# First-block loads and VectorE order, block 1's value weights, and the output's operand loads in an attention and expert-bottleneck kernel

## The chip, the cores and the metric

The kernel runs on one core of a Trainium2 chip. The metric is the device time of one execution in microseconds, taken as the median of several runs. The engines are TensorE (PE, its weight loads PEld), VectorE (DVE), ScalarE (ACT), GpSimd (POOL) and SyncE (SP), which here issues most DMAs; ScalarE issues the others on a queue of its own.

## The reference, cut to what matters

```python
x  = L0_attn_x                                # (2, 2048, 2048) float32, 4096 tokens
xn = (x - mean(x)) / sqrt(var(x) + 1e-5)
qkv = xn @ Wqkv + bqkv                        # Wqkv: 2048 x 1536; q, k, v of 512 each
out = softmax(q @ k.T / sqrt(512)) @ v        # for each of the 2 batches
attn = out @ Wo + bo                          # Wo: 512 x 2048
scores = (xn @ Wq_w.T) @ keys.T               # 16 router dimensions, 64 experts
gate = softmax over the 16 highest scores, zero elsewhere
z = (xn @ A_w.T) * gate                       # 64 experts x rank 8 = 512
result = x + attn + (z @ B_w.T) * 2.0
```

## The kernel before

All large products are float32 products made of three fp32r matmuls: each operand is split into a high part, which ScalarE casts (`split_hi`, L123), and a low part, the difference, which VectorE (or GpSimd, if told so) subtracts (`split_lo`, L126). `product` (L131) adds low x high, high x low and high x high into one PSUM bank. There are seven banks `acc` and one `misc`.

The 4096 tokens are eight blocks of 512, each of four row tiles of 128. Blocks 0 and 1 are computed directly; blocks 2 to 7 in three pairs (`phase`, seven products for eight); then come the scores and the weighted sums of attention, and last the output product in the same seven-product form, in 16 rounds q of seven steps (P1, P2, P6, P5, P3, P7, P4). Rounds 0 to 7 make the first 1024 output columns (p = 0), rounds 8 to 15 the other 1024 (p = 1).

**Block 0** (`first_block`, L321). TensorE is warmed with bf16 matmuls on a zero tile. For each row tile t: `load` brings 128 rows of x; `normal` takes statistics on VectorE (four `bn_stats`, L196, and one aggregate), then -mean (`nm`) and variance plus eps (`ve`), and GpSimd the reciprocal root (`rs`, L190); `scale` normalizes three quarters of the rows on VectorE (L351) and the fourth on ScalarE (L355, L356); `turn` transposes 16 squares of 128 on TensorE (L365) and splits them into `xh`. Value and router weights come as eight pieces (c2) of 256 rows for each half h of 264 columns (`wv_piece`, `weights`: load into `ws`, of which there are four buffers, high part, low part into `wh`, of which there are eight). `mul` (L378) is six matmuls 128x264 for one row tile and one piece. In the kernel before, the first half's pieces have their low parts on GpSimd; the first four are loaded by ScalarE's queue, the x rows by SP.

`values_out` (L274) empties a value bank: ScalarE copies the router's 16 columns (L282) and casts the high part (L286), VectorE subtracts (L287), and a store to DRAM is put down for later (`store`); `flush` issues what was put down. The buffers `vs` come from the ring `r_ev` of three.

**Block 1's values** (`values`, L299) run over the halves h, in each over the eight pieces, the two 128-row chunks of a piece and the four row tiles, one bank for each row tile. In the half h = 1 a step of block 2's statistics goes with each piece (`steps`: ScalarE's queue loads 1024 columns of x into one of three buffers `xs`, VectorE takes statistics).

**The feature tiles** of blocks 0 and 1 (L851 on) are 12 products of 48 matmuls each (`ftile`). At given tiles (`todo`, L862) they carry steps for later blocks, among them four loads of block 2's part of xT (`x_steps`, L628, 512 KB each).

**The output.** `moving(p, step, kk)` (L1064) returns a pair: `load`, which brings a step's weights into `r_wo` (two buffers) or, for the small steps of p = 1, `r_wo1` (four), and `split`, which makes high and low parts (`wb`) in the four slots of that step. Those slots are in use by the same step of the round before. `ahead` (L1209) prepares the other operand `s` three products ahead, `stationary` (L1112) with VectorE's sums and differences of `xz` (L1119 to L1124). `combine` (L1177): P1's bank is copied to `u` by ScalarE (L1182) and then P2 accumulates on the same bank.

What sets the order: each engine runs its instructions in the order in which the program was built, and a scheduler of the tile layer chose that order by estimated readiness when the kernel was built. `behind(key)` (L113) ties what is traced inside it behind a remembered instruction (`last[key]`) on that instruction's engine; instructions on other engines aren't tied. A DMA takes one of eight completion lanes in turn, and an issue waits for the DMA before it on its lane.

The lines that the change touches, beside those printed below:

```python
862            with behind("sp", "pe"):
863                for st in todo.get(k, []):
864                    st()
...
927    nc.vector.memset(mr32, 0.0)
930    nc.vector.memset(raw(mhl), 0.0)
932    nc.vector.tensor_tensor(pick, ...)
...
1300            m = n + 7 * q - 7 * (NG - 1)
1301            if 0 <= m < 7:
1302                more[m] = [moving(1, STEPS[m], kk) for kk in range(0, ND, 2)]
1303                for load, _ in more[m]:
1304                    load()
1305            if 1 <= m <= 7:
1306                with behind("act"):
1307                    for _, split in more[m - 1]:
1308                        split()
```

Of the kernel before, what the change touches and what calls it, by code (L numbers as in the profile page):

```python
# [34 lines left out]
def raw(ap):  # L35
    return ap.bitcast(F32)
# [27 lines left out]
def attn_ffn_kernel(ctx: ExitStack, tc, x, xT, wq, wv, wob, bqk, bv, bo, keysT, out):  # L64
# [57 lines left out]
    def split_hi(hi, src):  # L122
        return nc.scalar.copy(hi, src)  # L123
# [150 lines left out]
    def values_out(i, t, h, r, qr, ps, u=None):  # L274

        n0 = RD if h == 0 else 0
        at = 0 if h == 0 else VH - RD
        vs = r([P, 2, VH], FR, "vs")
        if u is None:
            v = ps  # L280
            if h == 0:
                nc.scalar.copy(qr[:, t, :RD], ps[:, :RD])  # L282
        else:
            v = raw(vs[:, 1, :])
            nc.vector.tensor_tensor(v[:, n0:], ps[:, n0:VH], u[:, n0:], ALU.add)
        split_hi(vs[:, 0, n0:], v[:, n0:VH])  # L286
        split_lo(vs[:, 1, n0:], v[:, n0:VH], vs[:, 0, n0:])  # L287
        store(v_d[i][t][:, :, at : at + VH - n0], raw(vs[:, :, n0:]))

    def wv_piece(h, c2, eng=None, queue=None):  # L290
        ch, cc = divmod(2 * c2, HC)
        return weights(wv[h, ch, :, cc : cc + 2, :], [2, VH], eng, queue)
# [6 lines left out]
    def values(i, xn, steps):  # L299
        qr = router_in()  # L300
        for h in range(2):
            ps = [acc() for t in range(NT)]
            for c2 in range(NCH // 2):
                wh = wv_piece(h, c2)
                for cc in range(2):
                    c = 2 * c2 + cc
                    for t in range(NT):
                        sl = slice(t * P, (t + 1) * P)
                        product(
                            ps[t][:, :VH], lambda a: xn[c][:, a, sl], lambda b: wh[:, b, cc, :],  # L310
                            c == 0, c == NCH - 1,
                        )
                if h == 1:
                    with behind("sp", "pe", "dve"):
                        steps[c2]()
            flush()
            for t in range(NT):
                values_out(i, t, h, r_ev, qr, ps[t])
        return qr

    def first_block():  # L321
# [8 lines left out]
        def load(t, cols):  # L330
            rows[t] = [xs0[2 * t + c]([P, 1024], F32, "xs") for c in range(2)]
            for c in range(2):
                for h in range(1024 // cols):
                    a = h * cols
                    nc.sync.dma_start(
                        rows[t][c][:, a : a + cols],
                        x[t * P : (t + 1) * P, c * 1024 + a : c * 1024 + a + cols],
                    )

        def normal(t):  # L340
            st = const.tile([P, 4, 6], F32, name="st6", bufs=2)
            row_stats(mv[:, t, :], rows[t], 0, st)
            nc.vector.tensor_scalar(nm[:, t : t + 1], mv[:, t, 0:1], -1.0, None, ALU.mult)
            rstd(rs[:, t : t + 1], mv[:, t, 1:2], 1)

        def scale(t):
            for n in range(4):
                c, h = divmod(n, 2)
                v = rows[t][c][:, h * 512 : (h + 1) * 512]
                if n < 3:  # L350
                    nc.vector.tensor_scalar(  # L351
                        v, v, mv[:, t, 0:1], rs[:, t : t + 1], ALU.subtract, ALU.mult
                    )
                else:
                    nc.scalar.activation(v, v, AF.Identity, bias=nm[:, t : t + 1])  # L355
                    nc.scalar.mul(v, v, rs[:, t : t + 1])  # L356

        def turn(t, g0=0, g1=NCH // 4):
            sl = slice(t * P, (t + 1) * P)
            for g in range(g0, g1):  # L360
                pt = acc()
                for j in range(4):
                    c = 4 * g + j
                    k = (c % 8) * P
                    nc.tensor.transpose(pt[:, j * P : (j + 1) * P], rows[t][c // 8][:, k : k + P], ident)  # L365
                for part in range(2):
                    for j in range(4):
                        hi, lo = (xn[4 * g + j][:, a, sl] for a in range(2))
                        pj = pt[:, j * P : (j + 1) * P]
                        if part == 0:  # L370
                            split_hi(hi, pj)
                        else:
                            split_lo(lo, pj, hi)

        def piece(c2, h, eng=None, queue=None):
            return wv_piece(h, c2, eng, queue)
# [11 lines left out]
        warm = half(0)([P, T], mybir.dt.bfloat16, "warm")  # L388
        nc.vector.memset(warm, 0.0)
        pw = misc()  # L390
        for j in range(20):
            nc.tensor.matmul(pw, warm[:, :P], warm, start=True, stop=True)
        load(0, 512)
        wh = [piece(c2, 0, nc.gpsimd, nc.scalar) for c2 in range(2)]
        normal(0)
        scale(0)
        load(1, 1024)
        turn(0, 0, 2)
        normal(1)
        turn(0, 2, 4)  # L400
        ps = [acc() for t in range(NT)]
        mul(ps[0], wh[0], 0, 0)
        mul(ps[0], wh[1], 0, 1)
        wh.append(piece(2, 0, nc.gpsimd, nc.scalar))
        mul(ps[0], wh[2], 0, 2)
        scale(1)
        wh.append(piece(3, 0, nc.gpsimd, nc.scalar))
        load(2, 1024)
        turn(1)
        for c2 in range(3):  # L410
            mul(ps[1], wh[c2], 1, c2)
        wh += [piece(c2, 0, nc.gpsimd) for c2 in range(4, N2)]
        load(3, 1024)
        constants()
        for c2 in range(3, N2):
            mul(ps[0], wh[c2], 0, c2)
            mul(ps[1], wh[c2], 1, c2)
            if c2 == 4:
                normal(2)
                scale(2)  # L420
                turn(2)
                normal(3)
        qr = router_in()
        for t in range(2):
            values_out(0, t, 0, r_ev, qr, ps[t])
# [405 lines left out]
    for i in range(2):  # L831
# [19 lines left out]
        for k, (fp, fh, summed) in enumerate(order):  # L851
# [43 lines left out]
    for j in PAIRS:  # L895
# [34 lines left out]
    nc.vector.memset(raw(mhl), 0.0)  # L930
    pick = const.tile([32 + NQ, NQ], F32, name="pick")
    nc.vector.tensor_tensor(
        pick, ident[: 32 + NQ, :NQ], ident[: 32 + NQ, 32 : 32 + NQ], ALU.add
    )

    def score(s):
        blk, k = divmod(s, NK)
# [338 lines left out]
    for q in range(2 * NG):  # L1276
# [4 lines left out]
        for n, step in enumerate(STEPS):  # L1281
# [69 lines left out]
```

## Time and profile before

| what | us |
|---|---|
| runs shown: lowest, median, highest of 3 | 2654.17, 2660.54, 2663.89 |
| the profiled execution's own time | 2656.96 |
| its span, first to last instruction | 2655.2 |
| VectorE busy in the span | 1807.5 |
| ScalarE busy in the span | 863.1 |
| GpSimd busy in the span | 569.6 |
| mean granted TensorE clock | 0.997 |

How to read it: a row of the timeline has the start, the duration, the engine, the line, the operation, what it writes and reads, how many instructions are merged, and in brackets how long the engine stood idle before it and what ended that. A row of the windows has a stretch, its length, the busy time (and number of instructions) of PE, PEld, VectorE, ScalarE and GpSimd, the granted clock of TensorE as a share of full speed, the mean busy share of the 16 DMA engines, and GB/s. Times are counted from the span's start. Beside the profile, the order in which the built programs hold each engine's instructions was read for both kernels; it has no times.

### The profile page before, as it was taken

The numbers are of one execution on the slowest core, as the hardware profiler recorded it, in microseconds if no ns is written. First come the engines' busy times: TensorE is split into PE (matmuls) and PEld (weight loads), VectorE is DVE, ScalarE is ACT, GpSimd is POOL, SyncE is SP. The second block draws the span as 40 slices with busy tenths as digits, with TensorE's granted clock in tenths as the row PEclk, the third lists the DMA queues.
The fourth block names the chain that finished last, engine by engine and source line by source line (L and its number), as shares of the span: only waits on it lengthen the run. The fifth ranks groups of instructions, "written<-read, shape, count | busy, mean of one in ns | idle before, by whom it ended". The sixth has DMA issues, their size and how long they took to land.

```text
span 2655.2 us, 33831 instructions
## 1 busy us (share of the span) xinstructions
PE 2628.8 (99%) x12875; PEld 2224.7 (84%) x12875; DVE 1807.5 (68%) x2487; ACT 863.1 (33%) x1285; POOL 569.6 (21%) x355
## 2 busy tenths in 40 slices
PE   8998999999999999999999999999999999999999
PEld 7888888888888888888888888888888888878887
DVE  6667738867878687756545675466568776797675
ACT  4232323333332333323233342334344222332221
POOL 2311420000000000000100101000002656556654
PEclk9999999999999999999999999999999999999999
DMA  6777775668546784536735476534368545565543
GB/s 232 252 259 264 269 264 201 212 211 298 194 143 220 233 299 137 175 115 213 289 116 178 155 254 237 206 119 143 125 202 270 172 161 165 181 212 174 178 158 105
DMA packets 243395, 530.42 MB, mean 200 GB/s; under 512 B 21608, under 2 KB 87200, under 8 KB 243232
## 3 DMA queue, kind: packets, MB, share of 16 engines
q1 hardware_dynamic: 229984, 497.81, 55.6%
q10 hardware_dynamic: 13248, 30.45, 3.3%
q8 instruction: 101, 1.65, 0.3%
q14 instruction: 62, 0.51, 0.1%
HBM read 393.80 MB, written 134.38 MB: 199 GB/s over the span
## 4 chain that ended last, share of the span: by engine, by line
PE 92%; DVE 4%; DMA 3%; issue 1%; ACT 0%; POOL 0%; SPq 0%; DVEq 0%; ACTq 0%; POOLq 0%
PE acc L131 69%; PE acc L1170 22%; DMA xs<-in_x 2%; DVE st L196 1%; DMA ws<-in_wv 1%; DMA xc<-in_xT 1%; DVE pw L126 1%; DVE xc L256 1%; DVE xq L655 1%; DVE wh L126 0%; DVE xc L257 0%; DVE t L126 0%; DVE wb L126 0%; DVE xs L351 0%; DVE s L126 0%
## 5 line engine op out<-in xcount | busy, mean ns | idle before, releaser
L131 PE MATMUL acc<-t,pw 128*128 128x512 f32 x3024 | 694.3, 390 | 1.1 <-DVE t L126 0.9
L131 PEld LDWEIGHTS acc<-t,pw 128*128 128x128 f32 x3024 | 565.3, 188 | 119.6 <-DVE t L126 1.8
L1170 PE MATMUL acc<-wb,s 128*128 128x512 f32 x2688 | 609.7, 389 | 2.6 <-ACT u L1182 2.6
L1170 PEld LDWEIGHTS acc<-wb,s 128*128 128x128 f32 x2688 | 504.6, 188 | 107.5 <-ACT u L1182 3.0
L131 PE MATMUL acc<-ph,vt 128*128 128x512 f32 x1536 | 367.5, 390 | 0.0
L131 PE MATMUL acc<-qt,kt 128*128 128x512 f32 x1536 | 366.0, 389 | 0.0
L131 PEld LDWEIGHTS acc<-ph,vt 128*128 128x128 f32 x1536 | 287.5, 188 | 62.1 <-DVE ot L1033 1.2
L131 PEld LDWEIGHTS acc<-qt,kt 128*128 128x128 f32 x1536 | 288.2, 188 | 60.2 <-issue 0.2
L1154 POOL TENSOR_TENSOR xo<-xo,bo_bc 128x512 f32<-128x512 f32 x128 | 212.6, 1667 | 560.4 <-DMA xo<-in_x 305.1
L123 ACT CAST pw<-pw 128x1024 fp32r<-128x1024 f32 (+1 forms) x168 | 177.6, 1058 | 378.9 <-PE acc L131 219.9
L131 PE MATMUL acc<-xh,wh 128*128 128x512 f32 x1152 | 263.6, 390 | 0.0
L126 DVE TENSOR_TENSOR pw<-pw 128x1024 fp32r<-128x1024 f32 (+1 forms) x168 | 217.2, 1293 | 67.5 <-ACT pw L123 67.1
L131 PEld LDWEIGHTS acc<-xh,wh 128*128 128x128 f32 x1152 | 215.6, 188 | 44.9
L131 PEld LDWEIGHTS acc<-pw,t 128*128 128x128 f32 x2016 | 245.8, 188 | 1.3
L131 PE MATMUL acc<-pw,t 128*128 128x264 f32 x2016 | 246.4, 283 | 0.0
L123 ACT CAST s<-xz 128x1024 fp32r<-128x1024 f32 x112 | 118.0, 1054 | 381.8 <-PE acc L1170 305.0
L126 DVE TENSOR_TENSOR s<-xz,s 128x1024 fp32r<-128x1024 f32 x112 | 168.0, 1500 | 43.9 <-ACT s L123 43.8
L126 DVE TENSOR_TENSOR ph<-sp,ph 128x512 fp32r<-128x512 f32 x128 | 94.2, 738 | 120.4 <-ACT ph L123 119.6
L957 DVE TENSOR_TENSOR M<-M,sp 128x512 f32<-128x512 f32 x112 | 79.3, 708 | 124.1 <-ACT sp L951 123.6
L525 POOL TENSOR_TENSOR zt<-zt,g 128x512 f32<-128x512 f32 x24 | 34.3, 1441 | 494.6 <-DMA g<-gd 203.8
L951 ACT COPY sp<-acc 128x512 f32<-128x512 f32 x128 | 74.8, 585 | 183.2 <-PE acc L131 183.1
L126 DVE TENSOR_TENSOR wh<-wu,wh 128x512 fp32r<-128x512 f32 x96 | 85.4, 906 | 70.5 <-ACT wh L123 70.5
(150 smaller groups left out, 2383.7 us busy)
## 6 DMA issues: line engine op xcount, KB each, us to landing
vt<-v_d SPq DMA_DIRECT2D x128, 512.0 KB, 3.5
pw<-sq_d SPq DMA_DIRECT2D x72, 512.0 KB, 3.7
xz<-oz_d SPq DMA_DIRECT2D x64, 512.0 KB, 4.9
xo<-in_x SPq DMA_DIRECT2D x128, 256.0 KB, 3.5
out_y<-xo SPq DMA_DIRECT2D x128, 256.0 KB, 2.3
pw<-in_wq SPq DMA_DIRECT2D x54, 512.0 KB, 3.7
wu<-in_wq SPq DMA_DIRECT2D x48, 512.0 KB, 7.0
xq<-in_xT SPq DMA_DIRECT2D x48, 512.0 KB, 5.7
```

Of the source, the lines that this page charges most:

```text
L123: return nc.scalar.copy(hi, src)
L126: return (eng or nc.vector).tensor_tensor(lo, src, raw(hi), ALU.subtract)
L131: last["pe"] = nc.tensor.matmul(ps, st(a_), mv(b_), start=first and n == 0, stop=end and n == 2)
L196: nc.vector.bn_stats(st[:, parts, :], xt[:, h * 512 : (h + 1) * 512])
L256: nc.vector.tensor_tensor(xc, xc, mb[:, 0, :], ALU.subtract)
L525: nc.gpsimd.tensor_tensor(zt, zt, gx[n], ALU.mult)
L655: eng.tensor_tensor(xg[(j, *to, cp)], xg[(j, *x0, cp)], xg[(j, *x1, cp)], op)
L951: nc.scalar.copy(st, ps)
L957: nc.vector.tensor_tensor(M[blk], M[blk], st, ALU.max)
L1154: nc.gpsimd.tensor_tensor(xs, xs, bo_bc[q // (NB // 2 * NH), c], ALU.add)
L1170: nc.tensor.matmul(ps, st[a_][:, kk, sl], mv[b_], start=not more and kk == 0 and n == 0, stop=kk == ND - 1 and n == 2, skip_group_check=more,)
```

## The change

In block 0 the second half of the first row tile's columns is loaded by ScalarE's queue, 26 warm-up matmuls take the place of 20, the low parts of pieces 0 to 5 are subtracted by VectorE (6 and 7 still by GpSimd), and the order on VectorE is written out with `behind`. In block 1 the pieces of the second half, but for the first, are tied behind the last eviction of the first half. The steps of `todo` are also tied behind the last issued store. Three small VectorE operations for attention are tied behind the last weight subtraction. In the output, the weights of the second column half are loaded two products before they are split.

```diff
@@ values_out
-        split_hi(vs[:, 0, n0:], v[:, n0:VH])
+        last["ev"] = split_hi(vs[:, 0, n0:], v[:, n0:VH])
@@ values
-                wh = wv_piece(h, c2)
+                with behind(*(["ev"] if h == 1 and c2 else [])):
+                    wh = wv_piece(h, c2)
@@ first_block: load, normal, scale, turn
-                    nc.sync.dma_start(
+                    (nc.scalar if t == 0 and c else nc.sync).dma_start(
...
-            nc.vector.tensor_scalar(nm[:, t : t + 1], mv[:, t, 0:1], -1.0, None, ALU.mult)
+            last["nm"] = nc.vector.tensor_scalar(nm[:, t : t + 1], mv[:, t, 0:1], -1.0, None, ALU.mult)
...
-                    nc.vector.tensor_scalar(
+                    last["row"] = nc.vector.tensor_scalar(
...
-                            split_lo(lo, pj, hi)
+                            last["row"] = split_lo(lo, pj, hi)
@@ first_block
-        for j in range(20):
+        for j in range(26):
             nc.tensor.matmul(pw, warm[:, :P], warm, start=True, stop=True)
         load(0, 512)
-        wh = [piece(c2, 0, nc.gpsimd, nc.scalar) for c2 in range(2)]
+        wh = [piece(0, 0, None, nc.scalar)]
         normal(0)
+        with behind("nm"):
+            wh.append(piece(1, 0, None, nc.scalar))
         scale(0)
         load(1, 1024)
         turn(0, 0, 2)
-        normal(1)
+        for c2 in range(2, 4):
+            with behind("row"):
+                wh.append(piece(c2, 0, None, nc.scalar))
         turn(0, 2, 4)
         ps = [acc() for t in range(NT)]
-        mul(ps[0], wh[0], 0, 0)
-        mul(ps[0], wh[1], 0, 1)
-        wh.append(piece(2, 0, nc.gpsimd, nc.scalar))
-        mul(ps[0], wh[2], 0, 2)
+        for c2 in range(3):
+            mul(ps[0], wh[c2], 0, c2)
+        with behind("row"):
+            normal(1)
+        with behind("nm"):
+            wh += [piece(c2, 0) for c2 in range(4, 6)]
         scale(1)
-        wh.append(piece(3, 0, nc.gpsimd, nc.scalar))
         load(2, 1024)
+        for c2 in range(3, 6):
+            mul(ps[0], wh[c2], 0, c2)
         turn(1)
-        for c2 in range(3):
+        for c2 in range(6):
             mul(ps[1], wh[c2], 1, c2)
-        wh += [piece(c2, 0, nc.gpsimd) for c2 in range(4, N2)]
+        with behind("row"):
+            wh += [piece(c2, 0, nc.gpsimd) for c2 in range(6, N2)]
         load(3, 1024)
         constants()
-        for c2 in range(3, N2):
+        for c2 in range(6, N2):
             mul(ps[0], wh[c2], 0, c2)
             mul(ps[1], wh[c2], 1, c2)
-            if c2 == 4:
-                normal(2)
+            if c2 == 6:
+                with behind("row"):
+                    normal(2)
                 scale(2)
                 turn(2)
-                normal(3)
+                with behind("row"):
+                    normal(3)
@@ feature tiles
-            with behind("sp", "pe"):
+            with behind("sp", "pe", "store"):
@@ before attention
-    nc.vector.memset(mr32, 0.0)
+    with behind("dve"):
+        nc.vector.memset(mr32, 0.0)
...
@@ output
             if 0 <= m < 7:
-                more[m] = [moving(1, STEPS[m], kk) for kk in range(0, ND, 2)]
-                for load, _ in more[m]:
+                with behind("act"):
+                    for _, split in more.pop(m):
+                        split()
+            if -2 <= m < 5:
+                more[m + 2] = [moving(1, STEPS[m + 2], kk) for kk in range(0, ND, 2)]
+                for load, _ in more[m + 2]:
                     load()
-            if 1 <= m <= 7:
-                with behind("act"):
-                    for _, split in more[m - 1]:
-                        split()
```

The memset of `mhl` and the operation `pick` (L930, L932) are tied in the same way as `mr32`.

More of the change, by code (lines that the diff above doesn't have):

```diff
@@ L926, in attn_ffn_kernel @@
     mr32 = const.tile([P, 32], F32, name="mr32")
-    nc.vector.memset(mr32, 0.0)
+    with behind("dve"):
+        nc.vector.memset(mr32, 0.0)
     mrT = const.tile([P, 32], F32, name="mrT")
     mhl = const.tile([32 + NQ, 32], FR, name="mhl")
-    nc.vector.memset(raw(mhl), 0.0)
+    with behind("dve"):
+        nc.vector.memset(raw(mhl), 0.0)
     pick = const.tile([32 + NQ, NQ], F32, name="pick")
-    nc.vector.tensor_tensor(
-        pick, ident[: 32 + NQ, :NQ], ident[: 32 + NQ, 32 : 32 + NQ], ALU.add
-    )
+    with behind("dve"):
+        nc.vector.tensor_tensor(
+            pick, ident[: 32 + NQ, :NQ], ident[: 32 + NQ, 32 : 32 + NQ], ALU.add
+        )
     def score(s):
```

## The prediction

> **What bounds it now.** I read the page's first part, then what TensorE waited for, then windows and timeline around those waits.
>
> ```profile
> PE 2628.8 (99%) x12875; PEld 2224.7 (84%) x12875; DVE 1807.5 (68%) x2487; ACT 863.1 (33%) x1285; POOL 569.6 (21%) x355
> ```
>
> TensorE is busy 99% of the span, so a change that removes no matmul can win only TensorE's idle time and its slow clock. The list of what PE waited for (total us, times, longest) gives the places:
>
> ```profile
> PE acc L131 <- DVE vs L126: 9.4, 1, 9.4
> PE acc L365 <- DVE xs L351: 7.6, 3, 6.3
> PE acc L1170 <- ACT u L1182: 2.6, 1, 2.6
> ```
>
> They are block 1's second value half (at 229 us), the first row tile, and the output's second product of q = 8 (at 2349 us). The change touches all three. The windows (PE busy, PEld, DVE, ACT, POOL, granted clock, DMA share, GB/s) show that a long wait also costs clock:
>
> ```profile
> 6.00:8.00 2.00, 1.86 (x9) 0.66 (x7) 1.38 (x2) 0.74 (x2) 2.00 (x2) 1.00 1.09 402
> ...
> 12.00:14.00 2.00, 0.00 (x0) 0.00 (x0) 2.00 (x4) 0.00 (x0) 1.22 (x2) 0.62 1.01 411
> ```
> ```profile
> 233.00:236.00 3.00, 0.00 (x0) 0.00 (x0) 2.81 (x5) 1.67 (x6) 0.00 (x0) 0.72 0.95 338
> 236.00:239.00 3.00, 0.22 (x1) 0.22 (x2) 2.97 (x8) 1.22 (x6) 0.00 (x0) 0.50 0.89 307
> 239.00:242.00 3.00, 3.00 (x14) 3.00 (x15) 2.93 (x8) 0.37 (x1) 0.00 (x0) 0.50 0.88 296
> 242.00:245.00 3.00, 3.00 (x17) 3.00 (x16) 0.91 (x3) 0.62 (x1) 1.81 (x2) 0.57 0.67 207
> ```
>
> A mean of 0.72 over 3 us is 1.7 us at half clock, 0.57 is 2.6: the clock was half from 234.3 to 244.6, having fallen 5.0 us after TensorE stopped at 229.3. Likewise it fell 4.6 us after the warm-up matmuls end (7.87), at 12.5, and came back at 19.3.
>
> **Part 1, block 1 (values_out, values).** The timeline:
>
> ```profile
> 235.56 0.37 ACT L123 CAST vs<-acc 128x248 fp32r<-128x248 f32 x1
> ...
> 238.78 6.39 PE L131 MATMUL acc<-wh,xh 128*128 128x264 f32 x29 [9.44 <-DVE vs L126]
> ...
> 241.32 0.37 ACT L123 CAST vs<-acc 128x248 fp32r<-128x248 f32 x1 [4.10 <-DMA v_d<-vs]
> ```
>
> The second half's first nine matmuls use three spare banks; the fourth must be evicted. In the built order ScalarE has six weight casts of the second half ahead of the evictions, each waiting for its load, so the eviction starts at 235.5. In the changed order the four evictions come directly behind the first cast. Bank 0 is complete 9 matmuls (1.1 us) before the first half's end; copy, cast and VectorE's subtraction take 0.9 us (50.17 to 51.07 for the same operations in block 0). The bank is then free when it is needed. Removed: 9.44 us idle, and of the 5.8 us from 238.78 to 244.6 at half clock half, 2.9 us: 12.3.
>
> What is late next is the second piece. Its cast now stands behind the fourth eviction, whose buffer is the first's (three slots) and waits for the first's store: issue to cast took 238.75 to 241.32, 2.57 us. Counted from the first half's end: store issued at 0, fourth cast 2.6 to 3.0, weight cast 0.63 to 3.6, subtraction 0.70 to 4.3. TensorE wants it after 24 matmuls of 0.1216 (201 took 24.44), 2.9. New wait 1.4 us, too short for the clock. Later pieces cost VectorE 0.70 + two statistics 1.28 + 0.13 = 2.1 us against TensorE's 2.9. The four 512 KB loads of xT that lay among these weights (209 to 219 us) go behind a store, two feature tiles later; four tiles of 10.9 us lie before their use, so they cost nothing; without that room, one landing (5.7 us on the page). **Gain 12.3 - 1.4 = 10.9**; ends 7 (store landing in 5 us) and 12.3.
>
> **Part 2, the first row tile.**
>
> ```profile
> 13.63 1.43 DVE L351 TENSOR_SCALAR xs<-xs,mv,rs 128x512 f32<-128x512 f32 x3
> 14.20 3.27 PEld L365 LDWEIGHTS acc<-ident,xs 128*128 128x128 f32 x16 [6.84 <-DVE xs L351]
> 14.21 3.67 PE L365 MATMUL acc<-ident,xs 128*128 128x128 f32 x16 [6.34 <-DVE xs L351]
> ...
> 15.36 3.34 ACT L123 CAST xh<-acc 128x128 fp32r<-128x128 f32 x16 [3.68 <-PE acc L365]
> ```
>
> Before, the four quarters landed at 4.8, 6.0, 7.3, 8.6, each beside a weight piece; 0.53 MB per 1.3 us is what the DMA gives. Now quarters share that rate with quarters: all in by 6.0, statistics end at 7.8 instead of 9.8, and the statistics of tile 1 no longer stand before the scaling. But two weight subtractions, new on VectorE, do. Their pieces come behind the quarters, beside 512 KB rows on the other queue. Their queue's share is not shown there; where such pairs run together (231 to 233 us) I read some 0.4. Pieces land at 7.8, 9.8, 11.7, 13.3 (with half: the last at 12.0; with a third: 14.6). Second piece 9.8 + cast 0.63 + subtraction 0.70 = 11.1, scaling 0.57: first transpose 11.7 instead of 14.2. The warm-up, six more at 0.21, ends at 9.15: 2.5 us idle, clock kept.
>
> Then it is given back. ScalarE's fourth weight cast stands before the sixteen xh casts: 13.3 + 0.63 = 13.9 (15.36 before). VectorE starts 0.8 later, 16 x 0.20 + two weight pieces 1.3: 19.2, where before it ended at 19.7. Only now come tile 1's statistics (four 2.46, then 0.5), two more pieces 1.3, scaling 0.6: tile 1's transposes run from 24.1 to 26.0; before, they ended at 26.8. Gain so far 0.8 (2.1 with half, -0.6 with a third). POOL's rs(1) stands behind pieces 6 and 7 there, whose loads are last in the queue; done near 22.9, covered by the 23.5; if they land 2 us later, tile 1 slips by 1.4.
>
> Next, tile 3. VectorE's new order puts the eviction of ps[2] before tile 3's nm and ve. All of ps[2] must therefore finish first, and TensorE has nothing else queued before tile 3's transposes. From the end of ps[2]: 0.15 + eviction 0.9 + nm, ve 0.2 + POOL 0.65 + scaling 0.6 = 2.5 us idle, where before matmuls of ps[2] covered the same chain. Against some 0.3 us of small waits saved there: -2.2. **Part 2: 0.8 - 2.2 = -1.4**; ends -5 (third share, and half clock, below) and +5 (transposes 2.5 earlier plus half of 14.2 to 19.3, nothing given back).
>
> One new gap may cost clock. Tile 0's matmuls with pieces 4 and 5 wait for VectorE from about 18.3 (pieces 2 and 3 done at 17.6, six matmuls each) to 22.9: 4.6 us, and the clock fell 4.6 and 5.0 us after work stopped. I count it as not falling; if it falls, it stayed half for 5.1 and 5.8 us after work resumed, 2.9 at most, some 2 beside the other waits. [...]
>
> On the two queues the rows show both busy from the start (share 1.09, 402 GB/s); only who goes first changes. [...]
>
> **Part 3, output.**
>
> ```profile
> 2348.29 1.72 DVE L1122 TENSOR_TENSOR xz<-xz 128x1024 f32<-128x1024 f32 x1
> ...
> 2350.11 1.04 ACT L123 CAST s<-xz 128x1024 fp32r<-128x1024 f32 x1 [9.72 <-DVE xz L1122]
> 2351.07 1.07 ACT L1182 COPY u<-acc 128x512 f32<-128x512 f32 x2
> ...
> 2351.70 4.61 PE L1170 MATMUL acc<-wb,s 128*128 128x512 f32 x19 [2.56 <-ACT u L1182]
> ```
>
> The bound is VectorE's backlog (3.00 of 3.00 in every window from 2329), not loads: from 2285 on VectorE waited 0.2 us for a weight cast and for no load. The built order moves the first u copy ahead of the s cast, so P2's first tile starts on time; the second stays behind it. VectorE's L1122 moves behind four halves of P7's weights, one of P4's and a finish. Net from the end of P3's weights (2342.7, less 2.4 for three operations that moved behind it): 11.2 us of listed work, L1122 from 2351.5 to 2352.8, cast 1.05, copy 0.6: P2's second tile near 2354.7 instead of 2351.9. Tile 2 would before have started at 2351.7 + 2.73 = 2354.4. **About -0.7** with some POOL overlap (ops of 1.2 stretch to 2.2 here); ends +2.6 (wait gone) and -4: on SP the loads of a step now wait for the split two products back, before the xo loads and the stores of out, and VectorE, which waited 1.8 us for xo here, would wait for those.
>
> The three memsets and pick go from the first 13 us to before attention: 1.1 us on an engine at 68%, nothing; at worst 1.1.
>
> **Sum.** 10.9 - 1.4 - 0.7 = 8.8 us. The profiled execution took 2656.96 (span 2655.2 and 1.8 around it): 2648.2. It lies 3.6 under the median of the runs shown, 2660.54; the forecast is for that median: **2651.7**.
>
> **Rivals.** (a) The start does pay: pieces land at equal share, little is given back, +4, and the output breaks even: gain 15, 2645.5. For: everything on VectorE is ordered for tile 0. Against: the tile-3 wait above. (b) More is given back: the 4.6 us gap halves the clock (-2) and the store lands late in block 1 (-3.5): gain 3.3, 2657.2. (c) Slower: block 1's pieces become a serial loop. Each x load now stands between two weight casts on ScalarE and waits for statistics of a load three back; before, casts came at 222.5, 226.0, 229.2, 3.3 us apart, with DMA at 1.05. If a loop takes 5 us against TensorE's 2.9, seven pieces lose 14.7, and net with parts 2 and 3 it is 12.3 - 14.7 - 2.1 = -4.5: 2665.0. It decides from 4.4 us a piece on. Against: the xT loads are gone from there, so 0.79 MB a piece needs 2 us. (d) That the order is not what the diff says: excluded by the built order.
>
> **Chances.** Forecast 0.53 (2648 to 2656), (a) 0.25, (b) 0.15, (c) 0.06, rest 0.01. For 8 in 10: 2643 to 2658. Half a per cent, 13.3 us, is about what a measurement of this kernel can tell from no change: faster 0.24 (most of (a)), same 0.72, slower 0.04 (the far end of (c)).
>
> **What would show it.** No PE wait on vs L126 at 229 and no half clock there; one of 1 to 2 us soon after. First transpose near 11.7, tile 1's ending near 26, a PE wait of 2 to 3 us on tile 3's scaling; P2's second output tile waiting on u. Wrong if pieces land much earlier than 13, if tile 3 does not wait, or if any new wait passes 4.6 us.

## The result, and the profile after

The changed kernel took 2662.2 us (median of 22 runs, 2657.3 to 2667.45); the kernel before took 2656.84 in as many (2653.66 to 2663.89). The ratio is 1.0017, with a 95% interval of 1.001 to 1.0024: some 3 to 6 us slower, where 8.8 us less had been forecast, and 4 us above the range. The forecast stood on the median of the three runs known then, 2660.54; on the median of all 22 it would have been 2648.0. Measured against the 0.5% bound the result is no change; against its own interval it is a small loss.

The profiled execution has a span of 2661.1 us (2655.2 before). The engines' line of its page, and then the list of what TensorE waited for (total us, times, longest):

```profile
PE 2632.8 (99%) x12881; PEld 2227.1 (84%) x12881; DVE 1818.6 (68%) x2493; ACT 863.4 (32%) x1285; POOL 569.7 (21%) x349
```
```profile
PE acc L1184 <- ACT u L1196: 7.7, 1, 7.7
PE acc L366 <- DVE xs L352: 5.1, 1, 5.1
PE acc L131 <- DVE wh L126: 4.6, 1, 4.6
PE acc L366 <- issue: 2.4, 1, 2.4
PE acc L131 <- ACT t L123: 1.8, 1, 1.8
```

The wait of 9.4 us in block 1 is gone. In its place the output's wait has grown from 2.6 to 7.7, the first row tile has a second wait of 4.6, and two smaller ones are new. TensorE is also "busy" 4.0 us more. The 26 warm-up matmuls took 7.24 us, the 20 before 6.68: 0.6 of that. A matmul at half clock counts as busy for nearly twice as long (before, 26 of 128x264 took 5.50 us from 239.0 on at half clock, 85 took 10.00 from 206 on at full: 0.21 and 0.12 each); TensorE worked 18.0 us at half clock, against 10.9 before, and half of the difference, 3.5, is about the rest.

Both traces hold every matmul, so the start of the n-th one behind the warm-up can be compared between them. This splits the 5.9 us between the two executions by place:

| from, to | difference at the end of the stretch | in the stretch | forecast |
|---|---|---|---|
| start to tile 3's transposes (42.31 us before, 49.00 after) | +6.7 | +6.7 | +1.4 |
| to block 1 at full clock (244.63, 240.22) | -4.4 | -11.1 | -10.9 |
| to pair 1's second product at full clock (537.7, 536.6) | -1.1 | +3.3 | 0 |
| to the output's q = 8, ahead of its wait (2345.1, 2343.8) | -1.4 | -0.3 | 0 |
| to the end | +5.9 | +7.3 | +0.7 |

Block 1, in the timeline (start, duration, engine, line, operation, and in brackets the idle time ahead and what ended it):

```profile
237.57 0.37 ACT L123 CAST vs<-acc 128x248 fp32r<-128x248 f32 x1 [2.26 <-DMA v_d<-vs]
...
238.52 11.66 PE L131 MATMUL acc<-wh,xh 128*128 128x264 f32 x92 [0.53 <-ACT wh L123]
```

The fourth eviction waits for the first's store, as forecast, and the weight cast behind it makes TensorE wait; but for 0.53 us, not 1.4.

The first row tile, in the same view:

```profile
9.72 0.63 ACT L123 CAST wh<-ws 128x528 fp32r<-128x528 f32 x1 [2.84 <-DMA ws<-in_wv]
...
13.55 3.67 PE L366 MATMUL acc<-ident,xs 128*128 128x128 f32 x16 [5.13 <-DVE xs L352]
...
21.30 2.46 DVE L196 BATCH_NORM_STATS2 st<-xs 128x6 f32<-128x512 f32 x4
...
24.23 2.01 DVE L126 TENSOR_TENSOR wh<-ws,wh 128x528 fp32r<-128x528 f32 x2
...
25.67 2.79 PE L131 MATMUL acc<-wh,xh 128*128 128x264 f32 x11 [4.64 <-DVE wh L126]
...
28.26 3.48 PE L366 MATMUL acc<-ident,xs 128*128 128x128 f32 x16
```

The first weight piece is cast at 9.7 instead of the forecast 7.8, and the transposes come at 13.55 instead of 11.7. Pieces 4 and 5, cast by 19.9, are subtracted from 24.2 on, behind tile 1's statistics, and the first of the two takes 1.39 us, where the two at 18.48 took 0.70 each, while GpSimd's subtraction for piece 7 runs until 25.06 beside it; TensorE stands for 4.64 us until then. Sixteen transposes take 3.5 us at 28.26 where 1.9 is usual: the clock is half. The windows (PE busy, PEld, DVE, ACT, POOL, granted clock, DMA share, GB/s) show it there and in the output:

```profile
21.00:25.60 4.60, 0.03 (x1) 0.00 (x0) 4.53 (x11) 1.99 (x3) 3.10 (x3) 0.90 0.41 124
25.60:31.50 5.90, 5.83 (x28) 5.83 (x28) 3.35 (x12) 2.71 (x12) 0.44 (x1) 0.50 0.94 308
...
2350.00:2358.00 8.00, 0.51 (x3) 0.08 (x1) 8.00 (x6) 1.34 (x2) 6.57 (x5) 0.66 0.36 131
```

In the first row VectorE is busy 4.53 of 4.60 us and the DMAs are at 0.41: the list, not a load, holds TensorE. The last row says the same of the output, with GpSimd busy beside VectorE. What TensorE waits for there is the forecast chain, the second copy to `u` behind the cast of `s`, and that cast behind VectorE's sum of `xz` (L1136; L1122 in the kernel before):

```profile
2356.66 1.05 ACT L123 CAST s<-xz 128x1024 fp32r<-128x1024 f32 x1 [10.89 <-DVE xz L1136]
2357.61 0.58 ACT L1196 COPY u<-acc 128x512 f32<-128x512 f32 x1
...
2358.24 17.12 PE L1184 MATMUL acc<-wb,s 128*128 128x512 f32 x65 [7.74 <-ACT u L1196]
```

### The profile page after: what moved, and what is told of

It is laid out like the page before. It is cut to its first block, busy times and chain, and to the rows that moved or that the text cites. A ratio compares the mean times of both kernels' runs of the same rounds, so it can differ in the third digit from the quotient of the medians.

```text
span 2661.1 us, 33841 instructions
## 1 busy us (share of the span) xinstructions
PE 2632.8 (99%) x12881; PEld 2227.1 (84%) x12881; DVE 1818.6 (68%) x2493; ACT 863.4 (32%) x1285; POOL 569.7 (21%) x349
## 4 chain that ended last, share of the span: by engine, by line
PE 95%; DVE 2%; DMA 2%; issue 1%; ACT 0%; ACTq 0%; SPq 0%; DVEq 0%
PE acc L131 73%; PE acc L1184 22%; DMA xs<-in_x 1%; DVE wb L126 1%; DMA ws<-in_wv 0%; DVE st L196 0%; DVE pw L126 0%; PE acc L366 0%; DVE xq L666 0%; DMA wo<-tw_d 0%; DVE xo L1173 0%; PE misc L466 0%; PE misc L999 0%; DVE xh L126 0%; DVE wh L126 0%
## 5 line engine op out<-in xcount | busy, mean ns | idle before, releaser
L126 DVE TENSOR_TENSOR wh<-wu,wh 128x512 fp32r<-128x512 f32 x96 | 96.1, 1025 | 64.9 <-ACT wh L123 64.9
```

What stands on the lines that cost most here:

```text
L126: return (eng or nc.vector).tensor_tensor(lo, src, raw(hi), ALU.subtract)
```

## The experiments

The theory after the result: the three parts are independent and add; the start loses by its queue's share, by VectorE's order and by the clock; the output loses because VectorE's list reaches one sum of `xz` later. Times are medians; ratios are against runs of the kernel before on the same chip.

| run | us | ratio, 95% interval |
|---|---|---|
| e1: block 1's part alone | 2646.59 | 0.9959, 0.9947 to 0.9972 |
| e2: first block's part alone | 2668.1 | 1.0042, 1.003 to 1.0055 |
| e3: output's part alone | 2663.24 | 1.0024, 1.0015 to 1.0033 |
| e4: block 1's part and the store tie | 2645.63 | 0.9956, 0.9943 to 0.9968 |
| e5: changed kernel, pieces 4, 5 first | 2659.41 | 1.0004, 0.9996 to 1.0013 |
| e6: changed kernel, pieces on one queue | 2656.41 | 0.9995, 0.9986 to 1.0004 |
| e7: changed kernel, no bias at q = 8 | 2656.82 | 1.0, 0.9992 to 1.0009 |
| e8: e4, longer warm-up, late cast | 2651.2 | 0.9979, 0.997 to 0.9988 |
| e9: changed kernel, splits one product later | 2655.17 | 0.9986, 0.9977 to 0.9995 |
| e10: e4 with a repaired first block | 2646.93 | 0.9958, 0.9946 to 0.9971 |
| e11: e10 with four low parts on GpSimd | 2641.13 | 0.9941, 0.9929 to 0.9954 |
| e12: the changed kernel once more | 2661.55 | 1.0014, 1.0005 to 1.0024 |

### The parts, each alone (e1 to e4)

e1 is the kernel before with this alone:

```diff
-        split_hi(vs[:, 0, n0:], v[:, n0:VH])
+        last["ev"] = split_hi(vs[:, 0, n0:], v[:, n0:VH])
...
-                wh = wv_piece(h, c2)
+                with behind(*(["ev"] if h == 1 and c2 else [])):
+                    wh = wv_piece(h, c2)
```

> Block 1's part alone: the weight pieces of its second half stand behind the last eviction, nothing else of the change. In the two profiles the changed kernel won 11.1 us between matmul 1250 and matmul 1277 (block 1) and lost 3.4 again at about 531 us, where pair 1's second product starts (1.8 + 0.9 us of waits and a stretch of 3.41 us at half clock). Theory: the win is block 1's alone, and the loss at 531 us is what VectorE and the loads take back from any kernel that arrives early there: no wait over 1.5 us at 229 us, a wait of 1 to 3 us near 530 us, and 7 to 9 us less than before (ratio 0.997). Rival A: the loss at 531 us comes from the moved xT loads, which this kernel doesn't have: 10 to 12 us less (0.9958). Rival B: without the room in the queue that the moved xT loads made, a weight piece comes late and block 1 itself waits some 5.7 us again: 2 to 6 us less.

Measured 2646.59, ratio 0.9959: Rival A's number. Between the same two matmuls in block 1 its profile gains 11.1 us, the wait there is 0.60 us, and nothing is lost near 530 us. So the loss of 3.3 at that place is not what any kernel that arrives early gives back, as the theory had it, and rival B falls too: the xT loads may stay where they were.

e2 is the kernel before with all that the change's diff has under `first_block`, and nothing else:

```diff
+                    (nc.scalar if t == 0 and c else nc.sync).dma_start(
...
+        for j in range(26):
...
+        wh = [piece(0, 0, None, nc.scalar)]
...
+        with behind("row"):
+            normal(1)
+        with behind("nm"):
+            wh += [piece(c2, 0) for c2 in range(4, 6)]
```

> The first block's part alone (row quarters on two queues, 26 warm-up matmuls, VectorE's subtractions and order). In the two profiles it lost 6.7 us by the end of tile 3's wait: first transpose only 0.7 earlier, then 4.6 us without matmuls and half clock from 24.6 to 31.5 us, then 2.1 us before tile 3. Theory: the loss is its own: 5 to 7 us more than before (ratio 1.002 to 1.0026), less up to 1.4 of it if the small waits at 534 us vanish. Rival: most of it was where the clock's windows happened to fall in that one execution: 1 to 3 us more (1.0008), with no half clock after 24 us in this profile.

Measured 2668.1, ratio 1.0042: more than the theory's 5 to 7. The start lost 6.4 us by tile 3's transposes, as in the changed kernel, with half clock again (from 23.8 to 30.6 us). The rest comes later: 1.1 in block 1, whose wait became 10.3, 1.5 at pair 1's second product (a wait of 1.6 us on `t`), and 1.6 from half clock behind the output's old wait.

e3 is the kernel before with the output's hunk of the diff alone:

```diff
             if 0 <= m < 7:
-                more[m] = [moving(1, STEPS[m], kk) for kk in range(0, ND, 2)]
...
+                with behind("act"):
+                    for _, split in more.pop(m):
+                        split()
+            if -2 <= m < 5:
+                more[m + 2] = [moving(1, STEPS[m + 2], kk) for kk in range(0, ND, 2)]
```

> The output's part alone (weights of the second column half loaded two products ahead). In the two profiles it lost 7.0 us: TensorE waits 7.74 us for the first product's copy of q = 8 (2.56 before) and runs at half clock for some 4.5 us behind that. Theory: VectorE's sums of xz come later because their order now has six halves of weights ahead of them and GpSimd's bias adds run beside these, so the loss is the edit's own: 5 to 9 us more than before (ratio 1.002 to 1.003). Rival: the loss came from the 3 to 4 us that the changed kernel is ahead there, with the loads where they were: 0 to 2 us more.

Measured 2663.24, ratio 1.0024, and a wait of 7.9 us for u: the theory. The kernel is not ahead there (2.6 us behind in this profile), so the loss doesn't come from being early.

e4 is e1 with one more line:

```diff
-            with behind("sp", "pe"):
+            with behind("sp", "pe", "store"):
```

> Block 1's part and the tie of the steps behind the last store (which moves four 512 KB loads of xT from among block 1's weights to the feature tiles). Theory: the tie is worth nothing either way: within 1.5 us of the kernel with block 1's part alone, and the same wait near 530 us. Rival A: the tie is what loses at 531 us: 3 to 4 us slower than block 1's part alone. Rival B: the tie makes room for the weights: 3 to 6 us faster than block 1's part alone.

Measured 2645.63, 1.0 us below e1, with intervals that overlap: the tie is worth nothing that these runs can tell, and both rivals fall. This kernel has the moved xT loads and loses nothing near 530 us, so e1's Rival A had the right number for a wrong reason; of the parts alone, only e2 has the long wait on `t`. The three parts add: -0.44% (e4), +0.42% (e2), +0.24% (e3) make +0.22%; measured +0.17%.

### What the start loses by (e5, e6)

```diff
         with behind("row"):
-            normal(1)
-        with behind("nm"):
             wh += [piece(c2, 0) for c2 in range(4, 6)]
+        with behind("dve"):
+            normal(1)
```

> The changed kernel with one swap: the low parts of weight pieces 4 and 5 on VectorE go ahead of tile 1's statistics instead of behind them. In the changed kernel their casts were done at 19.9 us, but the subtractions ran from 24.2, behind 2.46 us of statistics, and TensorE stood from 21.0 to 25.7. Theory (order on VectorE is the cause of that gap and of the half clock behind it): TensorE goes on at about 22.5 with pieces 4 and 5, waits some 3 us for tile 1's transposes, which start near 27 instead of 28.3, and the clock does not fall after 24 us, or falls for one 3.4 us stretch at most: 2.5 to 5 us less than the changed kernel. Rival (the late weight loads are the cause): the subtractions start no earlier than 23.5 even so, and the time moves by less than 1 us.

Measured 2659.41, 2.8 below the changed kernel (3.5 in the profile). TensorE goes on at 22.45, and the clock, back at full from 17.1 us, doesn't fall again before the output (2351.8):

```profile
22.45 2.87 PE L131 MATMUL acc<-wh,xh 128*128 128x264 f32 x18 [1.02 <-DVE wh L126]
25.59 0.87 PE L131 MATMUL acc<-wh,xh 128*128 128x264 f32 x5 [0.28 <-POOL wh L126]
27.95 2.01 PE L366 MATMUL acc<-ident,xs 128*128 128x128 f32 x16 [1.49 <-DVE xs L352]
```

The order of VectorE's list made that gap and the half clock; the transposes, late by 0.9 against the expectation, now take 2.01 us.

e6 puts the first four pieces on SyncE's queue, with tile 1's rows behind them:

```diff
-        wh = [piece(0, 0, None, nc.scalar)]
+        wh = [piece(0, 0, None, nc.sync)]
...
-            wh.append(piece(1, 0, None, nc.scalar))
+            wh.append(piece(1, 0, None, nc.sync))
         scale(0)
-        load(1, 1024)
         turn(0, 0, 2)
...
-                wh.append(piece(c2, 0, None, nc.scalar))
+                wh.append(piece(c2, 0, None, nc.sync))
+        load(1, 1024)
```

> The changed kernel with the first four weight pieces on SyncE's queue, ahead of tile 1's rows, instead of on ScalarE's queue beside them. In the changed kernel ScalarE's queue got a third of the bytes (0.13 of 0.41 MB a microsecond from 8 to 13 us) and the pieces were cast at 9.7, 11.7, 13.6, 15.6. Theory (the share of the queues made the first row tile late): pieces 0 and 1 are cast by 8.8, the first transpose comes at 10.3 to 11.3 instead of 13.55, and tile 0's first matmuls at 14 instead of 17.2; tile 1's rows come 3 to 4 us later, which its statistics (21.3 in the changed kernel) hardly notice. Time 0 to 3 us less than the changed kernel, as the gap behind tile 0 gets longer. Rival (VectorE's order or ScalarE's, not the loads, held the first transpose): it stays at 13 or later.

Measured 2656.41, 5.8 below the changed kernel, more than expected. The timeline of TensorE:

```profile
9.82 2.01 PE L366 MATMUL acc<-ident,xs 128*128 128x128 f32 x16 [1.36 <-DVE xs L352]
11.90 1.86 PE L131 MATMUL acc<-wh,xh 128*128 128x264 f32 x13
13.98 1.70 PE L131 MATMUL acc<-wh,xh 128*128 128x264 f32 x12 [0.23 <-DVE wh L126]
19.85 2.79 PE L131 MATMUL acc<-wh,xh 128*128 128x264 f32 x11 [4.16 <-DVE wh L126]
```

The first transposes are 3.7 us earlier and at full clock: the loads held them. The gap behind tile 0 is as long as ever (4.16), since VectorE's list is unchanged. The gain isn't the start's alone: this profile, 4 us under the run's median, is 10.5 us shorter than the changed kernel's, 6.0 of them by tile 3's transposes and 3.7 at 531 us, where this kernel lost nothing.

### What the output loses by (e7, e9, e8)

e7 leaves the bias out of the rows of q = 8:

```diff
-        nc.gpsimd.tensor_tensor(xs, xs, bo_bc[q // (NB // 2 * NH), c], ALU.add)
+        if q != NG:
+            nc.gpsimd.tensor_tensor(xs, xs, bo_bc[q // (NB // 2 * NH), c], ALU.add)
```

> The changed kernel without the addition of the bias bo to the output rows of round q = 8 (GpSimd's L1168 there; that part of the result is left out). In the changed kernel VectorE's operations of 0.64 and 1.2 us took 1.45 and 2.3 us at 2344 to 2358 us while GpSimd added biases for 8.5 and 4.1 us. Theory (contention with GpSimd lengthens VectorE's list ahead of the sum L1136): VectorE's operations there take 0.65 and 1.2 us again, L1136 ends some 5 us earlier, the wait for u falls from 7.7 us to 2 to 3 us, no half clock there: 5 to 7 us less than the changed kernel. Rival (the list's order alone does it): the wait stays above 6 us.

Measured 2656.82, 5.4 below the changed kernel, with a wait for u of 3.3 us. The same operations on VectorE's timeline, first in the changed kernel and then in this one:

```profile
2344.01 5.78 DVE L126 TENSOR_TENSOR wb<-wo,wb 128x512 fp32r<-128x512 f32 x4
...
2353.16 2.28 DVE L126 TENSOR_TENSOR wb<-wo,wb 128x1024 fp32r<-128x1024 f32 x1
2355.36 1.21 DVE L1136 TENSOR_TENSOR xz<-xz 128x1024 f32<-128x1024 f32 x1
```
```profile
2347.24 2.49 DVE L126 TENSOR_TENSOR wb<-wo,wb 128x512 fp32r<-128x512 f32 x4
...
2351.98 1.21 DVE L126 TENSOR_TENSOR wb<-wo,wb 128x1024 fp32r<-128x1024 f32 x1
2353.11 1.22 DVE L1136 TENSOR_TENSOR xz<-xz 128x1024 f32<-128x1024 f32 x1
```

Beside GpSimd's additions four halves take 5.78 us, without them 2.49. The theory holds but for one number: half clock came all the same (2355.3 to 2362.1). In this profile, the slowest of its runs, the output loses 3.6 us instead of 7.3; it loses 5.0 at 531 us.

e9 keeps early loads, one product ahead of the kernel before's instead of two, but splits where that kernel did:

```diff
-            if 0 <= m < 7:
+            if 1 <= m <= 7:
                 with behind("act"):
-                    for _, split in more.pop(m):
+                    for _, split in more.pop(m - 1):
                         split()
-            if -2 <= m < 5:
-                more[m + 2] = [moving(1, STEPS[m + 2], kk) for kk in range(0, ND, 2)]
-                for load, _ in more[m + 2]:
+            if -1 <= m < 6:
+                more[m + 1] = [moving(1, STEPS[m + 1], kk) for kk in range(0, ND, 2)]
+                for load, _ in more[m + 1]:
                     load()
```

> The changed kernel with the output's weights loaded one product ahead and split one product later, where the kernel before split them; so the loads stay early, but VectorE's list has its sum L1136 ahead of four halves and two whole weight splits again, as before the change. Theory (the splits a product earlier are what pushed that sum back, and GpSimd's contention only stretches them): the wait for u falls from 7.7 us to 2 to 3.5, no half clock there, 5 to 7 us less than the changed kernel. Rival (the loads' place on SyncE's queue, which holds up the xo loads, or contention alone): the wait stays above 6 us and the time within 2 us of the changed kernel's.

Measured 2655.17, 7.0 below the changed kernel; the wait is the old one:

```profile
PE acc L1184 <- ACT u L1196: 2.8, 1, 2.8
```

In its profile the output loses 0.3 us. So loads one product early did no harm; the early splits did. Each of the two answers alone (e7, e9) takes the wait back to some 3 us: more work ahead of the sum, each piece of it stretched by GpSimd.

e8 leaves the change and tries cheaper answers on top of e4. Its core:

```diff
-        for j in range(20):
+        for j in range(46):
...
+        with behind("row", "rhi0"):
+            scale(1)
...
+        if q == NG and step == "P6":
+            late.append((hi, lo, src))
+            return
...
+            if late and n == 0:
+                hi, lo, src = late.pop()
+                with behind("act"):
+                    split_hi(hi, src)
+                split_lo(lo, src, hi)
```

> Not the changed kernel: the kernel before with block 1's part and the store tie, and two cheaper answers to the other two gaps. At the start 46 warm-up matmuls instead of 20, so that TensorE does not stop at 7.9 us, with tile 1's scaling tied behind tile 0's low parts; in the output, P6's cast of q = 8 is tied behind P1's copies to u, with the loads as they were before. Theory (clock, and the order of cast and copies, are what these two places cost): no half clock from 12 to 19 us, 2 to 3 us won at the start; the wait of 2.1 to 2.7 us for u at 2340 us gone: 4 to 6 us less than the kernel with block 1's part and the tie, so 15 to 17 less than before (ratio 0.994). Rival: the product P6 or P2 waits as long for something else of VectorE's list, and the output part wins nothing: 2 to 3 us less, ratio 0.9948.

Measured 2651.2, 5.6 worse than e4: both expectations missed. ScalarE's copies were in time, and the wait moved to the next product and grew:

```profile
PE acc L1177 <- DVE s L126: 6.8, 1, 6.8
```

VectorE's list was again what was late: three halves of weights had come ahead of P6's operand, 4.57 us beside GpSimd. The warm-up kept the clock up to 838 us, but tiles 2 and 3 were only some 0.9 us ahead of e4's, as the first transposes came 0.75 later; and 3 us were lost at 835 to 841 us. That is the pattern of 531 us one pair of blocks later: in pair 2's second product TensorE waited 1.16 us for `t`, did one matmul, waited 0.91 again, and the clock was half from 837.9 to 841.3.

### A version that beats both (e10, e11), and the changed kernel again (e12)

e10 is the changed kernel with the output as before, e6's queue, e5's order, and

```diff
+        with behind("rs", "sa1"):
             wh += [piece(c2, 0, nc.gpsimd) for c2 in range(6, N2)]
...
-                with behind("row"):
-                    normal(3)
+                normal(3)
...
+        with behind("sc1", "sa1"):
+            for t in range(2):
+                values_out(0, t, 0, r_ev, qr, ps[t])
```

where `rs`, `sc1` and `sa1` are the root, VectorE's and ScalarE's scaling of tile 1.

> A version to beat both: block 1's part, the store tie and the moved memsets as changed; the output as before; the first block as changed, but with the first four weight pieces on SyncE's queue ahead of tile 1's rows, pieces 4 and 5 ahead of tile 1's statistics, tile 1's scaling ahead of the value evictions, GpSimd's root of tile 1 ahead of pieces 6 and 7, and tile 3's statistics free of their tie. Theory (each cause found so far is its own and they add): first transposes at 9.8 us, the gap behind tile 0 under 3 us without half clock, no idle time ahead of tile 3's transposes: the start 3 to 6 us shorter than before, block 1 some 11, so 2640 to 2644 us (ratio 0.993 to 0.995). Rival (what is won at the start is given back at 531 us or by a clock that falls elsewhere): no faster than the kernel with block 1's part and the tie, 2645.6.

Measured 2646.93: the rival. No time is idle ahead of tile 3's transposes any more, but tile 1's wait for VectorE (3.2 us, and one window at half clock) takes most of the 4.2 us that the first transposes are ahead of e4's, and a wait on `t` of 1.5 us with half clock at 523 us takes the rest.

```diff
-                wh.append(piece(c2, 0, None, nc.sync))
+                wh.append(piece(c2, 0, nc.gpsimd, nc.sync))
...
-        with behind("row"):
-            wh += [piece(c2, 0) for c2 in range(4, 6)]
-        with behind("dve"):
+        wh += [piece(c2, 0, nc.gpsimd) for c2 in range(4, 6)]
+        with behind("row"):
             normal(1)
```

> The version to beat both once more: as the last one, but the low parts of weight pieces 2 to 5 on GpSimd again (1.28 us each there, 0.66 on VectorE), where the kernel before had them. In the last version VectorE was busy without a gap from 11.3 to 19.4 us, so tile 1's transposes came at 21.25 with 3.2 us of waiting and 3.4 us at half clock behind it. Theory (VectorE's list is what binds the first 25 us once the loads are in): tile 1's statistics start near 14.7, its transposes at 18.5 to 19.5, no half clock behind the start, tile 3 as before: 2 to 4 us less than the last version, 2642 to 2645. Rival (GpSimd's subtractions, at twice the time, are late for TensorE, or lengthen VectorE's operations beside them): TensorE waits over 2 us for pieces 4 and 5 and nothing is won.

Measured 2641.13, ratio 0.9941: 5.8 below e10, more than the theory's 2 to 4 (the two intervals overlap a little), and 21 below the changed kernel. Between the two profiles the start is 3.5 us shorter, as the theory had it; another 2.4 come at 520 us, where e10 had its wait on `t` and half clock. TensorE's longest waits left in it:

```profile
PE acc L366 <- DVE xs L352: 2.5, 4, 1.1
PE acc L1183 <- ACT u L1195: 1.9, 1, 1.9
```

Tile 1's transposes start at 19.29, and the clock stays full from 7.0 to 2334.9 us.

e12 has no edit.

> The changed kernel once more, unedited, for a second profile. Theory: what the program's order causes comes again in the same place and size: first transpose at 13.5 to 14.3, the gap of 4 to 5 us behind tile 0 with half clock, 2.4 us ahead of tile 3, 7 to 8.5 us for u. What depends on where the clock's windows of 3.41 us fall differs: the half clock at 533 us (1.6 us of its loss there) may be gone or longer. Rival: the loss at 531 us is as fixed as the others: 3.4 us again within 0.5.

Measured 2661.55. The first transposes came at 13.62, the gap was 4.7, tile 3's 2.4, the wait for u only 6.1. At 531 us the rival is right: 1.8 us again, and half clock from 532.9 to 536.3.

## Why the prediction was wrong

By the profiles the change lost 5.9 us where 8.8 were to be won. Of these 14.7, 6.6 are the output's, 5.3 the start's, and 3.3 stand at 531 us, which no term covered. The largest step that failed is the price of VectorE's list ahead of the output's sum.

**Block 1** (10.9) was right: 11.1 in the change's profile, 10.9 by e1's profile and 9.8 by its median. The new wait was 0.5 rather than 1.4, and no piece became a serial loop, so rival (c) has nothing for it.

**The start** (-1.4) lost 6.7. Three steps:

- "Pieces land at 7.8, 9.8, 11.7, 13.3": they were cast at 9.7, 11.7, 13.6 and 15.6. The spacing was right at first, the first landing 1.9 late. From 8 to 13 us ScalarE's queue moved 0.73 MB in 347 rows of 2112 B and SyncE's 1.34 MB in 327 rows of 4096 B: nearly as many rows there, and 0.65 of the bytes in the longer ones. I had used some 0.4 for ScalarE's queue, from a stretch with 154 short rows against 124 long ones; it was 0.35, and less still from 5.5 to 7 us, while the first piece came in (42 rows against 75). In the other two stretches the numbers of rows are further apart, so no share that holds everywhere was shown; e6 shows what it cost to have the pieces on a queue of their own, 3.7 us at the first transposes.
- "Clock kept" and "I count it as not falling": it fell at 11.0 and at 24.6, and stayed half until 17.8 and 31.5. I had read the rows of before as a delay of 4.6 and 5.0 us after TensorE stops. What the runs show in its place stands at the end. The two cost half of 13.55 to 17.82 and of 25.67 to 31.47, 2.1 and 2.9 us, of which the kernel before paid 2.5 too and the forecast had both at nothing. The start's worse end, -5, did count a third's share and the second of the two; the start lost more.
- The gap itself (4.6 forecast, 4.64 measured) and tile 3's wait (2.5 forecast, 2.4 by the profile) were right in size. The profile lists the latter as "issue", but its rows have the forecast chain: the eviction of ps[2] until 47.57, `ve` until 47.69, GpSimd's root until 48.32, the scaling from 48.36 and the transposes from 49.00; and in e10, where tile 3's statistics are free of their tie, the wait is gone. Rival (b) named the gap's half clock, at 2 us and 0.15; it should have been the forecast.

**The output** (-0.7) lost 7.3. The chain was the forecast one; the step that failed is "11.2 us of listed work", from the end of P3's weights to the start of the sum: the same list took 16.5 (2338.9 to 2355.4). I knew of the stretch, and had let 1.2 become 2.2 here and there; but GpSimd was busy for 6.57 of the last 8 us, and e7's list, without the bias additions, took 12.0 (2341.1 to 2353.1). So 4.4 us are contention with them, and the other 0.9 lie beside GpSimd's remaining work: two of the whole operations took 2.0 in e7 as well. Then a wait of 7.7 passes into half clock (2352.5 to 2362.8), at which TensorE worked 4.5 us: half of that, 2.3, more. The range's end for this part, -4, had no clock in it.

**What was not in the sum**: 3.3 us at 531 us. The wait on `t` there is 0.2 to 0.7 us in the kernel before, e1, e3 and e4, and 1.4 to 2.1 in seven of the ten kernels with an edited first block, but 0.2 in e6 and 0.6 in e11, and in e8 it came one pair later. (e3 lost 1.9 us there all the same, most of it by a window at half clock.) In the changed kernel a 512 KB load of `xs` ahead of it takes 5.3 us from issue to use (506.1 to 511.4), in the kernel before, at the same place, 3.5; its last 32 packets of 256 come over the last 2 us. Why isn't settled; half of the loss is again the clock (half from 533.2 to 536.6, 1.7 us by the same count).

The signs were right in all three parts. The chance of no change within 0.5%, 0.72, was the case that came, but by luck: it stood for a small gain, and what came was a gain of 11 and losses of 17 that nearly cancel. The range failed because the output's end had neither the full stretch by GpSimd nor a clock in it, the start's end left out the first half clock, and nothing stood for 531 us.

## What to carry to other kernels

Where one engine's list is full, moving work earlier on it delays something else by the same amount: find which operation ends up behind, and price the list with the durations it has beside the other engines, not alone (here 5.78 us for four halves beside GpSimd's additions, 2.49 without them). Before costing a wait of TensorE at its length, read what waits of that size did to the granted clock in the profiles at hand, and add it: here the waits of 4.64 and 7.74 us went with 6.83 and 10.24 us at half clock, which I put at 2.9 and 2.3 us more. A part of a change that wins should be run alone: here block 1's part with its tie was worth 0.44%, and the other two took 0.66% back.

## What the runs showed of the hardware

In the profiles of before and of the changed kernel the granted clock changed on a grid of 3.413 us: its stretches at half clock lasted 3.41, 6.83 or 10.24 us. The grid lay otherwise against the start in the two, with the first fall at 12.47 and at 10.99. Between its first rise and the kernel's end the clock fell six times. In the 3.41 us ahead of the fall TensorE had been busy for 0 and 0% (before, falls at 12.47 and 234.34) and for 25, 0, 38 and 41% (changed kernel, falls at 10.99, 24.64, 533.23 and 2352.53). The least busy such stretches behind which it was kept had 45% (changed kernel, from 45.12) and 54 and 57% (before, from 227.51 and 2347.19). It came back six times, each time behind a stretch with over 99%, and stayed half behind seven with 0 to 70%. (The busy times are the profile's, which models the ends of matmuls.) The stretch ahead of the return at 17.82 in the changed kernel held transposes for 2.8 of its 3.4 us; in e5 the clock was back at 17.1 us, ahead of the first product's matmul at 17.63. At 533.23 the fall came with no single long wait: the stretch ahead of it held the last 1.2 us of a wait of 1.80 and one of 0.91, with half a microsecond of work between them. My delay of 4.6 us, counted from one stop, would have missed this.

VectorE's subtraction of 128x512 took 0.62 us alone and 1.45 on average beside GpSimd's additions, 128x1024 1.21 and 2.28; GpSimd's addition took 1.26 to 2.27. Of the four of 128x512 from 2344.01 on, three took 1.8 us, each ending 0.55 us behind the GpSimd addition that was under way when it began; the one that began between two additions took 0.68. What makes them end so was not shown.
